# Four graph-attention layers on one core: a small sum moved from GpSimd to ScalarE, a third of one layer's gathers of late rows replaced by matmuls, and a group of transposes moved ahead in TensorE's order

## The chip, the cores and the metric

The kernel runs on one core of a Trainium2 chip. The metric is the device time of one execution in microseconds (us). Engines are named as the profile names them: PE is TensorE (PEld its weight loads), DVE is VectorE, ACT is ScalarE, POOL is GpSimd, and SP is the engine that issues most loads. Times inside an execution are counted from the start of its span.

## The reference, cut to what matters

Four layers follow one another on x, 4096 nodes with 256 features, and on one adjacency matrix (4096 x 4096, some eight neighbours and the node itself in a row). Each layer normalises x, applies max(., 0), and adds an attention result to x:

```python
# layer 0: 8 heads, a curvature term      logits_ij = leaky(e_l[i] + e_r[j]) + gate * curv_bias[i, j]
# layer 1: one head                       e_ij = leaky(a1.h_i + a2.h_j + b)
# layer 2: one head, softmax of e and of -e
attention          =  softmax(where(mask,  e, NEG), axis=1)
negative_attention = -softmax(where(mask, -e, NEG), axis=1)
new_h = concatenate([attention @ inp, negative_attention @ inp], axis=1) @ wtrans
x = x + elu(new_h)
# layer 3: 4 heads, scores h_i . h_j
```

The adjacency matrix is an input, so which rows take part is known only at run time.

## The kernel before, in words

**Lists and gathers.** Layer 0's part of the program reads the whole adjacency matrix (64 MB), packs it to keys and finds, for each tile of 128 nodes, up to 9 chunks of 128 neighbour rows (`EC` = 9). There are 32 tiles. For a tile, every layer fetches the chunks from a table in HBM, one indirect DMA on POOL's queue for each chunk (line 909, `gather`), into a buffer `g` of which there are six (`G`). Chunks 0 to 6 (`EARLY` = 7) reach only table rows below 3584 (`NE`), so they can be fetched as soon as tiles 0 to 27 of the layer before have stored their rows. Chunks 7 and 8 (`LATE` = 8) need the whole table. The node's own row comes as a plain DMA on SP's queue (line 923).

**Expanding instead of gathering.** Chunk 8 holds only rows of the last four tiles (3584 and up). Layers 1 and 3 don't gather it: `keep_late` (line 1676) keeps these 512 rows in SBUF as three bf16 parts, `go_to` (line 1684) has made a 0/1 matrix `to` for each tile, stored in `rows_of` beside the tile's other matrix, and `expanded` (line 1695) multiplies the two in twelve matmuls and copies the result into `g` on ACT. Layer 2 gathers all nine chunks. So there are 32 x (9 + 8 + 9 + 8) = 1088 gathers.

**Layer 0's score.** `before0` (line 1489) spreads a tile's own terms to its edges and writes them to `mine`; its last statement, lines 1503 to 1505, adds `noloop` to the 8 own terms of the node itself, on POOL. `score0` (line 1507) adds `mine` to the gathered terms on DVE (line 1512). `weigh0` (line 1537) weighs the rows on DVE, `attend0` sums them on PE (line 930), `finish0` and `rows1` (line 1563) make the table rows of layer 1.

**Layer 2's steps** are called by `run` (line 1714) in rounds: a pair (lag, step) means that round r runs the step for tile r - lag. In a round PE takes: `attend2` of tile r (28 matmul instructions, line 1921), `turn3` of tile r - 2 (line 865, two transposes), `turn_signed` of tile r - 1 (line 1943, four transposes, copied to `two_t` on ACT, line 1947), `rows3` of r - 2 (line 874) and `through_wt` of r - 1 (line 1956, eight matmuls). `weigh2` makes the weights `sw` on DVE (lines 1777 to 1908); `signed2` takes the reciprocal of attend2's sums (DVE), the factor `scale` (line 1932) and writes `two` on ACT (line 1936). `finish2` ends the tile on DVE, and `rows3` makes layer 3's table rows.

**What sets the order.** PE's order is the order of the program. The other engines' orders are chosen by the scheduler of the framework from a model of costs, so they can change with any edit; each engine then runs its own queue in order. PSUM banks for layer 2's small products (`pt`) number three.

Of the kernel before, what the change touches and what calls it, by code (L numbers as in the profile page):

```python
# [10 lines left out]
BF16 = mybir.dt.bfloat16  # L11
# [3 lines left out]
AF = mybir.ActivationFunctionType  # L15
OP = mybir.AluOpType
# [4 lines left out]
P = 128  # L21
C = 256
KC = C // P
H0, D0, CF = 8, 32, 6
# [673 lines left out]
EC = 9  # L698
HE = 5 * P
SELF = EC  # L700
KX = 8
LATE = EC - 1
EARLY = EC - 2
G = 6
BEHIND = 3
ROW0, ROW1, ROW3 = C + H0 + CF, C + 2, C
# [7 lines left out]
def gnn_lists(  # L714
# [27 lines left out]
    nc = tc.nc  # L742
    N = x_in.shape[0]
    NT = N // P
# [35 lines left out]
    def tile_rows(a, t):  # L780
        return a[t * P : (t + 1) * P, :]
# [24 lines left out]
    LB = (N - NE) // P  # L806

    rows_of = [
        dram.tile([P, 2, (EC + LB) * P], BF16, name=f"rows_of{t}") for t in range(0, NT, 2)
    ]  # L810
# [19 lines left out]
    rows12 = [const.tile([P, 2, ROW1], F32, name=f"row12_{i}") for i in range(2)]  # L830
# [47 lines left out]
    def upper(a):  # L878

        n = len(a.shape)  # L880
        two = a.bitcast(BF16)
        if n == 2:
            return two.rearrange("p (a two) -> p a two", two=2)[:, :, 1]
        return two.rearrange("p s (a two) -> p s a two", two=2)[:, :, :, 1]
# [5 lines left out]
    def fetch(pool, src, shape, name, dtype=F32, bufs=3):  # L890
        a = pool.tile(shape, dtype, name=name, bufs=bufs)
        nc.sync.dma_start(a, src)
        return a
# [13 lines left out]
    def gather(t, g, table, width, chunks):  # L907
        for c in chunks:
            last = nc.gpsimd.indirect_dma_start(  # L909
                out=g[:, c, :width], out_offset=None, in_=table[: NE if c < EARLY else N, :],  # L910
                in_offset=bass.IndirectOffsetOnAxis(ap=nbr[:, t, c : c + 1], axis=0),
            )
        return last
# [7 lines left out]
    def gather_late(t, g, table, width, chunks=range(EARLY, EC)):  # L921
        last = gather(t, g, table, width, chunks)
        nc.sync.dma_start(g[:, SELF, :width], tile_rows(table, t))
        return last
# [25 lines left out]
    def three(a):  # L950

        return a.rearrange("p (b c) k -> p b c k", c=3)


    with tc.tile_pool(name="keep", bufs=1) as keep, tc.tile_pool(
# [9 lines left out]
        g = g_pool.tile([P, EC + 1, ROW0], F32, name="g").rearrange("p c k -> p (c k)")  # L965
# [18 lines left out]
        for e, size in zip(enc, (1.0, 0.5)):  # L984
# [5 lines left out]
                op0=OP.mult, op1=OP.mult,  # L990
# [30 lines left out]
        for i, a_s in enumerate((ar_s, al_s)):  # L1021
            for k in range(KC):
                nc.vector.tensor_scalar(
                    am[:, k, i * H0 + k * nh : i * H0 + (k + 1) * nh], of_head, a_s[:, k : k + 1],
                    None, op0=OP.mult,
# [25 lines left out]
        to = keep.tile([P, 1], F32, name="to")  # L1051
# [7 lines left out]
        noloop = keep.tile([P, NT], F32, name="noloop")  # L1059
        wc_b = keep.tile([EC * CF, EC, H0], F32, name="wc_b")  # L1060
        own0 = keep.tile([P, NT, 3, H0 + CF], F32, name="own0")
# [427 lines left out]
        def before0(t):  # L1489

            ps = ps_b.tile([P, 3, 512], F32, name="pb")
            my = mine0[:, t % MINE, :]
            nc.any.tensor_copy(
                my[:, P:].rearrange("p (i v) -> p i v", i=3), upper(own0[:, t, :, :])
            )
            s_ps, parts = spread(ps, of0[t].pop("st"), my, P + 3 * V0)
            s = of0[t]["s"] = work.tile([P, EC, P], F32, name="s_f", bufs=3)
            nc.scalar.copy(three(s), s_ps)
            mine = of0[t]["mine"] = work.tile([P, EC + 1, V0], F32, name="mine")
            nc.vector.tensor_reduce(  # L1500
                three(mine[:, :EC, :]), parts.rearrange("p b c (i v) -> p b c v i", i=3), AX.X, OP.add
            )
            nc.gpsimd.tensor_scalar(
                mine[:, SELF, :H0], own0[:, t, 0, :H0], noloop[:, t : t + 1], None, op0=OP.add
            )

        def score0(t):
# [89 lines left out]
        for q, n in groups:  # L1597
            for t in range(q, q + n):
                last = at_piece((t // (RG // P) + 1) * per_r - 1) + 7 + 2.5 * (t % (RG // P))
# [5 lines left out]
        first = 17 + NE // P * T_ROWS  # L1605
# [26 lines left out]
    with tc.tile_pool(name="work", bufs=2) as work, tc.tile_pool(name="kept", bufs=1) as kept:  # L1632
# [43 lines left out]
        def keep_late(rows, width):  # L1676

            for b in range(0, LB, 2):
                n = min(LB, b + 2) - b
                row = rows[b // 2 - (LB + 1) // 2][:, 2 - n :, :]  # L1680
                rest = work.tile([P, 2, ROW1], F32, name="rest", bufs=1)[:, :n, :width]
                in_parts([late_rows[:, b : b + n, i, :width] for i in range(3)], row, rest)
# [12 lines left out]
        def expanded(t, of, width, pool, name):  # L1695

            to = of.pop("to")
            ps = bank(pool, name)[:, :width]
            for b in range(LB):
                for i in range(3):  # L1700
                    nc.tensor.matmul(  # L1701
                        ps, lhsT=to[:, b * P : (b + 1) * P], rhs=late_rows[:, b, i, :width],
                        start=(b == 0 and i == 0), stop=(b == LB - 1 and i == 2),
                    )
            nc.scalar.copy(of["g"][:, LATE, :width], ps)
# [5 lines left out]
        def by_slot(a):  # L1711
            return a.rearrange("p (c r) -> p c r", r=P)

        def run(table, width, x_of, steps, first=None, expand=False, rows=True):


            of, late = [{} for _ in range(NT)], {}

            def loads(t):
                two = t // 2 * 2  # L1720
                if t == two:
                    of[t]["ss"] = work.tile([P, 2, EC * P], BF16, name="ss", bufs=3)
                    if not first:
                        nc.sync.dma_start(of[t]["ss"], s_of[t // 2])
                of[t]["pair"] = of[two]["ss"]
                of[t]["s"] = by_slot(of[t]["pair"][:, t - two, :])
                if rows:
                    if t == two:
                        of[t]["sts"] = work.tile([P, 2, (EC + LB) * P], BF16, name="st", bufs=4)
                        if not first:  # L1730
                            nc.sync.dma_start(of[t]["sts"], rows_of[t // 2])
                    both = of[two]["sts"][:, t - two, :]
                    of[t]["st"], of[t]["to"] = both[:, : EC * P], both[:, EC * P :]
                if first:
                    marked(first, t, of[t]["st"])
                    go_to(t, of[t]["to"])
                    if t > two:
                        store(rows_of[t // 2], of[two]["sts"])
                four = t // XT * XT
                if t == four:  # L1740
                    of[t]["xs"] = fetch(work, rows_of_x(x_of, t), [P, XT, C], "x")
                of[t]["x"] = of[four]["xs"][:, t - four, :]
                of[t]["all_x"] = of[four]["xs"]

            def begin(t):
                with ExitStack() as queue:
                    if t - BEHIND in late:
                        queue.enter_context(tc.issue_after(late.pop(t - BEHIND).ins))
                    of[t]["g"] = gather_early(t, table, width, g_pool)

            def begin_late(t):
                last = gather_late(t, of[t]["g"], table, width, range(EARLY, LATE if expand else EC))
                if t < G - BEHIND:
                    late[t] = last

            def late_lag(t):

                return (-1, -2, -2, -3, -3)[t] if t < 5 else 2 - G

            steps = [(-3, loads), (2 - G, begin), (late_lag, begin_late)] + [  # L1760
                (lag, lambda t, f=f: f(t, of[t])) for lag, f in steps
            ]
            rounds = {}
            for lag, f in steps:
                for t in range(NT):
                    rounds.setdefault(t + (lag(t) if callable(lag) else lag), []).append((f, t))
            for r in sorted(rounds):
                for f, t in rounds[r] if r < NT else sorted(rounds[r], key=lambda s: -s[1]):
                    f(t)
# [11 lines left out]
        with tc.tile_pool(name="only1", bufs=2) as only, tc.tile_pool(name="l1_o", bufs=2, space=PSUM) as ps_o, tc.tile_pool(  # L1781
# [7 lines left out]
                    late_no[:, b : b + 1], number, float(NE + b * P), None, op0=OP.add  # L1789
                )  # L1790
            nc.vector.tensor_copy(col_late, nbr[:, :, LATE])
            keep_late([rows12[t // 2 % len(rows12)] for t in range(0, NT, 2)], ROW1)

            def expand1(t, of):
                expanded(t, of, ROW1, ps_e, "pe")
# [46 lines left out]
            def rows2(t, of):  # L1842
# [15 lines left out]
                    (3, give2), (0, weigh1), (2, finish1), (1, attend1), (-1, before1),  # L1858
                    (2, rows2), (-1, expand1),
                ],  # L1860
                first=only, expand=True,
            )

        HP = P // 2
# [13 lines left out]
        with tc.tile_pool(name="only2", bufs=2) as only, tc.tile_pool(name="l2_o", bufs=2, space=PSUM) as ps_o, tc.tile_pool(  # L1878
# [2 lines left out]
            small2 = bank(ps_m, "small2")  # L1881
            all_rows = kept.tile([P, C], F32, name="all_rows")
            nc.vector.memset(all_rows, 0.0)

            def weigh2(t, of):

# [89 lines left out]
            def rows3(t, of):  # L1976
# [19 lines left out]
                for k in range(K3):  # L1996
# [4 lines left out]
            run(  # L2001
                table2, ROW1, xs[1],
                [
                    (0, weigh2), (1, signed2), (2, finish2), (0, attend2), (2, turn3), (1, turn_signed),
                    (2, rows3), (1, through_wt),
                ],
                rows=False,
            )

            ps = bank(ps_t, "pt")[:, :C]  # L2010
# [5 lines left out]
        with tc.tile_pool(name="only3", bufs=2) as only, tc.tile_pool(name="l3_o", bufs=2, space=PSUM) as ps_o, tc.tile_pool(  # L2016
# [69 lines left out]
            def finish3(t, of):  # L2086
# [12 lines left out]
            run(  # L2099
                table3, ROW3, xs[2],  # L2100
                [(0, weigh3), (1, attend3), (-1, before3), (2, finish3), (-1, expand3), (-2, own_parts)],
                expand=True,
            )


# [2 lines left out]
            for i, v in enumerate(inv):  # L2108
# [8 lines left out]
                op0=OP.add, op1=OP.subtract,  # L2117
# [89 lines left out]
```

## Time and profile before

| | |
|---|---|
| median of 3 runs | 1580.23 us (1580.05 to 1581.6) |
| profiled execution: its own time, its span | 1580.64 us, 1578.8 us |
| busy: PE, DVE, ACT, POOL | 1275.2, 1147.6, 686.5, 1076.9 us |
| gathers (line 909): number, busy in all | 1088, 1048.8 us |
| layer 0's gathers: first starts, last ends | 109.43 us, 511.60 us |
| layer 1's gathers | 526.79 us to 852.66 us |
| layer 2's gathers | 852.96 us to 1215.43 us |
| layer 3's gathers | 1217.68 us to 1538.88 us |
| line 1503 (the sum on POOL) | 32 times, median 324 ns |

The profile is one execution. Its groups give, for a line of the kernel, the engine, the tiles written and read, how often it ran, its busy time and the idle time just before it with what ended that. A timeline lists an engine's instructions by time, with the idle time ahead of each in brackets. A table by stretches gives each engine's busy time in a part of the span, with the granted clock of PE. The chain of waits of the page reaches back only to 640 us, so for what lies before that the timelines are read. The first gather of a layer is told from its place in POOL's order (288, 256, 288 and 256 gathers).

### The profile page before, as it was taken

The page shows a single profiled execution, that of the slowest core. Times are in us where ns is not written, and L with a number is a line of the kernel's source. Part 1 is how long each engine was busy: PE and PEld are TensorE (multiplying, and loading weights), DVE is VectorE, ACT ScalarE, POOL GpSimd, SP SyncE. Part 2 cuts the span into 40 slices and gives each one's busy share as a digit, 9 for nine tenths or more (in the row PEclk, how much of TensorE's full clock was granted, in tenths as well). Part 3 has the DMA queues.
Part 4 walks back from the last instruction along what each step waited for, and adds up shares of the span by engine and source line. Part 5 has one row for each costly group of instructions (what it writes and reads, how often), then busy time and mean ns, then how long its engine had stood idle before and what let it go on. Part 6 is the DMA issues. An engine that isn't in the chain of part 4 may idle for free.

```text
span 1578.8 us, 24849 instructions
## 1 busy us (share of the span) xinstructions
PE 1275.2 (81%) x7529; PEld 1026.4 (65%) x7536; DVE 1147.6 (73%) x3171; ACT 686.5 (43%) x1801; POOL 1076.9 (68%) x1179
## 2 busy tenths in 40 slices
PE   5773878877887759867777399989989799999995
PEld 3442656656665648756665378877777588888884
DVE  6666978888885567766665167766666699999995
ACT  4665767787452355544432044443444411111220
POOL 2027767777677477777777777777777777777770
PEclk9965888788898989988888699999999999999998
DMA  8969879998565578877779657766666767777740
GB/s 284 303 232 330 293 262 304 334 329 269 126 156 155 159 230 248 261 225 225 232 221 295 195 163 216 210 201 191 193 207 185 224 207 244 247 252 245 241 123 20
DMA packets 165921, 356.67 MB, mean 226 GB/s; under 512 B 28177, under 2 KB 100241, under 8 KB 165777
## 3 DMA queue, kind: packets, MB, share of 16 engines
q0 software_dynamic: 52224, 145.30, 33.6%
q1 hardware_dynamic: 67970, 143.98, 27.0%
q10 hardware_dynamic: 45582, 65.71, 11.6%
q8 instruction: 62, 1.02, 0.3%
q14 instruction: 83, 0.67, 0.1%
HBM read 291.66 MB, written 63.21 MB: 225 GB/s over the span
## 4 chain that ended last, share of the span: by engine, by line
PE 25%; POOL 11%; DVE 8%; DMA 7%; issue 6%; ACT 2%; DVEq 0%; POOLq 0%; ACTq 0%
POOL g L909 11%; PE o L930 9%; DMA g<-table,nbr 7%; PE o L1921 6%; PE pv L2058 3%; PE pt L1956 3%; DVE g L2076 3%; PE pv L1701 2%; DVE sw L1899 1%; PE pt L874 1%; ACT two_t L1947 0%; DVE prod L1848 0%; PE pt L1943 0%; DVE s L1777 0%; PE pe L1701 0%
## 5 line engine op out<-in xcount | busy, mean ns | idle before, releaser
L909 POOL DMA_INDIRECT g<-table,nbr x1088 | 1048.8, 964 | 374.7 <-issue 300.3
L930 PE MATMUL o<-g,sw 128*128 128x257 f32 (+1 forms) x1216 | 301.0, 405 | 3.0 <-DVE sw L1823 3.0
L930 PEld LDWEIGHTS o<-g,sw 128*128 128x128 f32 x1216 | 243.9, 203 | 43.7 <-DVE sw L1823 3.4
L1921 PE MATMUL o<-g,sw 128*128 128x257 f32 x896 | 204.9, 387 | 25.5 <-issue 25.5
L1921 PEld LDWEIGHTS o<-g,sw 128*128 128x128 f32 x896 | 174.6, 195 | 52.1 <-issue 25.5
L930 PE MATMUL o<-g,s_f 128*128 128x264 f32 x576 | 152.6, 424 | 0.0
L930 PEld LDWEIGHTS o<-g,s_f 128*128 128x128 f32 x576 | 124.7, 216 | 27.3
L1204 ACT ACTIVATE mask<-adj,minus_half 128x1024 bf16<-128x1024 int32 x112 | 125.3, 1144 | 21.0 <-DMA adj<-in_adj_l 9.0
L2067 ACT ACTIVATE pm<-s 128x40 f32<-128x40 f32 x32 | 6.6, 208 | 226.9 <-DVE s L2065 212.5
L2058 PE MATMUL pv<-parts,st 128*128 128x256 bf16 x864 | 101.1, 275 | 1.5 <-DMA parts<-own 1.5
L2062 DVE TENSOR_TENSOR v<-pv,g 128x512 f32<-128x512 f32 (+1 forms) x160 | 90.7, 628 | 4.1 <-PE pv L2058 4.0
L2058 PEld LDWEIGHTS <-st 128*128 128x128 bf16 x864 | 84.9, 98 | 12.7 <-DMA parts<-own 1.9
L2076 DVE SCALAR_TENSOR_TENSOR g<-pm,g 128x2560 f32<-128x2560 f32 x32 | 90.3, 2823 | 2.6 <-ACT g L2072 2.0
L1537 DVE TENSOR_TENSOR g<-g,pt 128x2560 f32<-128x2560 f32 x32 | 90.0, 2813 | 0.4 <-ACT pt L1534 0.3
L1956 PE MATMUL pt<-wt_s,two_t 128*128 128x256 f32 x256 | 69.2, 418 | 20.8 <-ACT two_t L1947 20.5
L898 ACT ACTIVATE off<-place,minus 128x1152 bf16<-128x1152 f16 x64 | 80.0, 1250 | 7.4 <-DVE st L899 5.7
L1701 PEld LDWEIGHTS <-st 128*128 128x128 bf16 x768 | 74.1, 98 | 13.9
L2063 DVE TENSOR_REDUCE s<-v 128x36 f32<-128x2304 f32 x32 | 81.7, 2553 | 1.1
L865 PE MATMUL pt<-ident,r 128*128 128x128 f32 x192 | 43.1, 311 | 47.5 <-DVE r L845 35.8
L874 PE MATMUL pt<-wcat,hT 128*128 128x272 f32 (+1 forms) x256 | 76.0, 423 | 4.6 <-ACT hT L867 4.2
L1956 PEld LDWEIGHTS pt<-wt_s,two_t 128*128 128x128 f32 x256 | 49.9, 202 | 35.5 <-ACT two_t L1947 28.9
L865 PEld LDWEIGHTS pt<-ident,r 128*128 128x128 f32 x192 | 25.8, 157 | 63.4 <-ACT rstd L836 22.5
(360 smaller groups left out, 2259.7 us busy)
## 6 DMA issues: line engine op xcount, KB each, us to landing
adj<-in_adj_l SPq DMA_DIRECT2D x128, 512.0 KB
ss<-s_of SPq DMA_DIRECT2D x32, 576.0 KB
g<-table,nbr POOLq DMA_INDIRECT x1088
rows_of<-st ACTq DMA_DIRECT2D x16, 832.0 KB
st<-rows_of SPq DMA_DIRECT2D x16, 832.0 KB
x<-x SPq DMA_DIRECT2D x24, 512.0 KB
s_of<-ss ACTq DMA_DIRECT2D x16, 576.0 KB
table<-row ACTq DMA_DIRECT2D x32, 258.0 KB
```

The lines of the kernel that those rows point to most:

```text
L874: nc.tensor.matmul(pp, lhsT=hT[:, k, :], rhs=w[:, k, :], start=(k == 0), stop=(k == KC - 1))
L909: last = nc.gpsimd.indirect_dma_start(out=g[:, c, :width], out_offset=None, in_=table[: NE if c < EARLY else N, :], in_offset=bass.Indirec ...
L930: nc.tensor.matmul(o, lhsT=a, rhs=b, start=(i == 0), stop=(i == len(pairs) - 1))
L1204: nc.scalar.activation(m, a, AF.Sign, bias=minus_half, scale=1.0)
L1537: nc.vector.tensor_mul(gh, gh, w[:, :, :, None].to_broadcast([P, K, H0, D0]))
L1701: nc.tensor.matmul(ps, lhsT=to[:, b * P : (b + 1) * P], rhs=late_rows[:, b, i, :width], start=(b == 0 and i == 0), stop=(b == LB - 1 and i ...
L1921: nc.tensor.matmul(o, lhsT=sw[:, h, i].rearrange("p s r -> p (s r)"), rhs=g[:, c, : C + 1], start=(i == 0), stop=(i == HC + 1),)
L1956: nc.tensor.matmul(pp, lhsT=lhs[:, k, :], rhs=wt_s[:, k, :], start=(k == 0), stop=(k == 2 * KC - 1))
L2058: nc.tensor.matmul(pv[:, k, :], lhsT=st[:, (a + k) * P : (a + k + 1) * P], rhs=parts[:, i, :], start=(i == 0), stop=(i == 2),)
L2062: nc.vector.tensor_mul(v[:, a : a + n, :], pv[:, :n, :], g[:, a : a + n, :C])
L2063: nc.vector.tensor_reduce(s[:, :EC, :], heads(v, K3), AX.X, OP.add)
L2076: weighed3[t] = nc.vector.scalar_tensor_tensor(gh, w[:, :, :, None].to_broadcast([P, K, K3, D3]), -math.e, gh, op0=OP.add, op1=OP.mult,)
```

## The change

Three edits.

1. Layer 0's own term is computed by an ACT instruction (Identity with `noloop` as bias) in place of the one on POOL.
2. In layer 2, tiles with t % 3 == 1 (1, 4, ..., 31: eleven tiles) expand chunk 8 on PE and don't gather it. For this `keep_late` runs once more at the start of layer 2, on the last rows of layer 1; `to` is fetched for these tiles by a DMA of 128 x 512 bf16 on SP's queue, in the round three ahead; the twelve matmuls come last in the round two ahead, into a `pt` bank.
3. In layer 2's round `turn_signed` of the tile before stands ahead of `attend2`, and `through_wt` ahead of `rows3`.

```diff
-            nc.gpsimd.tensor_scalar(
-                mine[:, SELF, :H0], own0[:, t, 0, :H0], noloop[:, t : t + 1], None, op0=OP.add
+            nc.scalar.activation(
+                mine[:, SELF, :H0], own0[:, t, 0, :H0], AF.Identity, bias=noloop[:, t : t + 1],
+                scale=1.0,
             )
...
             def begin_late(t):
-                last = gather_late(t, of[t]["g"], table, width, range(EARLY, LATE if expand else EC))
+                last = gather_late(t, of[t]["g"], table, width, range(EARLY, LATE if expand(t) else EC))
...
-            keep_late([rows12[t // 2 % len(rows12)] for t in range(0, NT, 2)], ROW1)
+            last12 = [rows12[t // 2 % len(rows12)] for t in range(0, NT, 2)]
+            keep_late(last12, ROW1)
...
             nc.vector.memset(all_rows, 0.0)
+            keep_late(last12, ROW1)
+
+            def by_tensor(t):
+                return t % 3 == 1
+
+            def fetch_to(t, of):
+                if by_tensor(t):
+                    of["to"] = fetch(
+                        only, rows_of[t // 2][:, t % 2, EC * P :], [P, LB * P], "to", BF16, bufs=3
+                    )
+
+            def expand2(t, of):
+                if by_tensor(t):
+                    expanded(t, of, ROW1, ps_t, "pt")
...
-                    (0, weigh2), (1, signed2), (2, finish2), (0, attend2), (2, turn3), (1, turn_signed),
-                    (2, rows3), (1, through_wt),
+                    (0, weigh2), (1, signed2), (2, finish2), (1, turn_signed), (0, attend2), (2, turn3),
+                    (1, through_wt), (2, rows3), (-2, expand2), (-3, fetch_to),
                 ],
-                rows=False,
+                rows=False, expand=by_tensor,
```

In layers 1 and 3 `expand` becomes a function that is always true, which changes nothing there.

More of the change, by code (lines that the diff above doesn't have):

```diff
@@ L1712, in by_slot, with run @@
             return a.rearrange("p (c r) -> p c r", r=P)
-        def run(table, width, x_of, steps, first=None, expand=False, rows=True):
+        def run(table, width, x_of, steps, first=None, expand=lambda t: False, rows=True):
             of, late = [{} for _ in range(NT)], {}
@@ L1860, in gnn_lists @@
                 ],
-                first=only, expand=True,
+                first=only, expand=lambda t: True,
             )
@@ L2101, in gnn_lists @@
                 [(0, weigh3), (1, attend3), (-1, before3), (2, finish3), (-1, expand3), (-2, own_parts)],
-                expand=True,
+                expand=lambda t: True,
             )
```

## The prediction

> **What bounds the kernel now.** By the table of stretches PE looks like layer 2's bound (90 to 97% busy from 893 to 1200 us, POOL 76%). POOL's timeline, read next, says otherwise. Here layer 2's last gathers meet layer 3's first:
>
> ```profile
> 1213.23 0.95 POOL L909 DMA_INDIRECT g<-table,nbr  x1 [0.30 <-issue]
> 1214.48 0.95 POOL L909 DMA_INDIRECT g<-table,nbr  x1 [0.30 <-issue]
> 1217.68 0.94 POOL L909 DMA_INDIRECT g<-table,nbr  x1 [2.25 <-DVE r L845]
> ```
>
> A gather takes 0.95 us and the next follows 0.30 us later, whose releaser is "issue": nothing the profile shows is waited for. So 0.30 us belongs to a gather's price, 1.25 us, and POOL is full at "76%". Layer 2's 288 gathers run from 852.96 to 1215.43 without one longer gap: 362.5 us, 1.259 each. Layer 1's 256 (325.9 us) and layer 3's (321.2 us) run on in the same way. From 526.8 us to 1538.9 us POOL waits only about 2 us, above, for layer 2's tile 27 to store its rows. From about tile 13 on, attend2 starts follow POOL: from 1021.95 (tile 13) to 1224.11 (tile 31) one each 11.23 us, where nine gathers cost 11.3.
>
> Layer 0 is different. POOL ends there at 511.60 and layer 1's first gather starts at 526.79: it waits for tile 27's table rows, whose `rows1` ends at 523.01 (line 1563) and whose store is issued at 523.04. So compute sets that layer's end. DVE's and PE's timelines tell what it waited for:
>
> ```profile
> 491.72 0.22 DVE L1510 TENSOR_TENSOR d<-g,mine 128x54 f32<-128x54 f32 x1 [0.17 <-DVE e L1532]
> 499.95 0.24 DVE L1512 TENSOR_TENSOR e<-g,mine 128x80 f32<-128x80 f32 x1 [8.01 <-POOL mine L1503]
> 500.23 0.24 DVE L1513 SCALAR_TENSOR_TENSOR e<-e 128x80 f32<-128x80 f32 x1
> 500.38 2.81 DVE L1537 TENSOR_TENSOR g<-g,pt 128x2560 f32<-128x2560 f32 x1
> ```
>
> ```profile
> 505.45 0.66 PE L865 MATMUL pt<-ident,r 128*128 128x128 f32 x2 [7.88 <-DVE r L845]
> 506.04 0.70 PE L1524 MATMUL pt<-wc_b,d_t 54*128 54x72 f32 x2
> 506.67 1.25 PE L930 MATMUL o<-g,ident 128*128 128x264 f32 x2
> 507.71 6.06 PE L930 MATMUL o<-g,s_f 128*128 128x264 f32 x18
> ...
> 517.40 4.17 PE L930 MATMUL o<-g,s_f 128*128 128x264 f32 x18
> ```
>
> The sum on POOL takes 0.32 us, but it stands behind gathers in POOL's queue. DVE waits 8.01 us for it, everything behind it on DVE waits too, and PE stands 7.88 us; the 18 matmuls after that take 6.06 us instead of 4.17.
>
> **Part 1, the self term.** In all DVE waits for line 1503 five times:
>
> ```profile
> L1503 POOL TENSOR_SCALAR mine<-own,noloop x32: 297/324/876, 21.0 to 511.9; 128x8 f32<-128x8 f32 x32
> ...
> who waited for it (us, times):
>   DVE e L1512: 25.3, 5
> ```
>
> Two of the five (11.4 us, after 430 us) lie in the tail that ends layer 0, three (13.9 us) earlier. *Tail*: without the 8.01 us, e ends at 492.2, the weighing (2.81) at 495.2; attend of tile 26 ends at 495.93, finish0 takes 2.2 us of DVE after it, so PE's transposes start at 498.1 and the next attend, 1.22 us after them, at 499.3 instead of 506.67: 7.4 us. The attend is then as short as the others: 4.7 instead of 7.1 us, 2.4 more. Of the second stall (3.38 us at 476.75) PE shows waits of 1.44 and 0.96; I take half, 1.2. Tail: 11.0 us, between 0 and 13.8. The granted clock was 0.76 in the 10 us with PE's wait, 0.65 in the 8 us after it and 1.00 in the 16 us after those. The Trainium skill's page "TensorE: Matmul & The Clock Gate" (Part 1) says that an idle window of about 3.4 us halves the clock until some 3.4 us of work have passed; by its rule alone the slow matmuls would cost 1.7 us and not the measured 2.4, and the sum would be 0.7 smaller.
>
> *Earlier*, ACT, DVE and PE wait for one another around the adjacency pieces. The groups of four tiles end their ranking (line 1252) 54.5 and 53.0 us apart where stalls of 6.1 and 5.3 us lie, and 45.9 to 49.2 (mean 47.3) in the later four. That speaks for up to 13; against it, the DMA engines are 86 to 88% busy. A stall removed from one engine of a convoy is mostly found again at the next, so I take 3.5, a quarter; the ends are 13.9 and, for the 24 or so added ACT instructions of 0.26 us (the row of line 1283, same shape) all exposed, a loss of 6. POOL itself gains 0.23 us for each sum taken out between gathers, which the wait at 511.6 hides. Part 1: **14.5 us**. Everything after it starts that much earlier, since layer 1's gathers start with tile 27's store; their other condition, tile 31's rows before the 29th gather, has 8 us to spare.
>
> **Part 2, the expansion.** Eleven gathers leave POOL: 11 x 1.259 = 13.8 us. What it adds:
>
> ```profile
> L1701 PE MATMUL pe<-late_rows,st x384: 270/274/423, 563.9 to 849.7; 128*128 128x258 bf16 x192
> ...
> L1705 ACT COPY g<-pe x32: 353/374/382, 567.3 to 855.7; 128x258 f32<-128x258 f32 x32
> ```
>
> Twelve such matmuls stand in the chain of waits as 1.34 us: 11 x 1.34 = 14.7 us of PE, 0.46 a tile. ACT's eleven copies of 0.37 us and SP's eleven loads of 128 KB are hidden: ACT is 44% busy there, and SP runs over two rounds (20 us) ahead. Uncovered, the copies cost 4.1 us, the loads up to 2.8 each (the longer landings of gathers in the chain). `keep_late` is two times (ACT 0.61, DVE 0.69, ACT 0.62, DVE 0.69), 5.2 us; DVE idles 23.49 us until layer 2's first gathers land (892.31), and that hides it. The first attend (894.07) follows 30 gathers that stay.
>
> Does PE now set the pace? A round of layer 2, in the chain's order, is attend 6.07, turn3 0.22, turn_signed 0.44, rows3 1.13, through_wt 1.73: 9.59 us. With 0.46 it is 10.05, against POOL's 362.5 less 13.8 over 32, 10.90. PE begins late, since it fills while POOL is already 40 us in. From attend of tile 2 at about 912.8 (below), 29 rounds give tile 31 at 1204. By the gathers its score, now at 1218.67, comes at 1204.9 and the attend some 4.5 us later, 1209.4. So gathers still decide, by 5 us, and the whole 13.8 us arrive. It may not exceed this, since POOL then runs on into layer 3.
>
> **Part 3, the order.** Now, when a gather is late, `two` of the tile before waits on DVE behind the late tile's weights, `two_t` waits behind `two` in ACT's queue, and PE waits for it before it can start the late attend:
>
> ```profile
> PE o L1921 <- issue: 25.5, 1, 25.5
> PE pt L1956 <- ACT two_t L1947: 19.1, 11, 2.3
> ```
>
> The 25.5 us are the layer's start, before the first attend. In the new order the 19 us go. What is late next is `two` itself, ahead of turn_signed: it ends 2.1 us after an attend where gathers are early (939.75 to 941.84), and turn3, through_wt and rows3 (3.08 us) cover it; 4 to 4.5 us where they are late, when PE waits for the gather anyway. At the layer's start nothing covers it: tile 1's attend starts 2 us later and tile 2's at 912.8, not 914.06. Since POOL sets the pace, I count part 3 as nothing for the end (between a loss of 2 and a gain of 1). It keeps PE from becoming the bound. `rows3` of tile 27, which layer 3's first gather awaits, moves behind through_wt, 1.3 us later in its round; attend being up to 14.7 us earlier, the gather is still 13.8 earlier.
>
> **Sum.** 1580.64 (the profiled execution; its span 1578.8 and 1.8 around it) - 14.5 - 13.8 = 1552.3; that execution is 0.4 above the median of the runs, so I say **1552**. Layer 3 keeps its length: PE and DVE are 98% busy there from 1350 to 1450, and it moves as one piece.
>
> **Rivals.**
> *A, the self term waits on ACT instead.* ACT runs its queue in order, and in 100 to 430 us it stood 43.4 us (15 times, at most 6.5) for PE ahead of line 1563. If the new instruction sits behind such a wait, DVE's 25.3 us come back. For: ACT waited some 98 us there in all. Against: the copy `s_f` just before it in the program is seldom late (2.3 us of DVE waits). Time: 1580.6 - 13.8 = 1567. The Trainium skill's page "TensorE: Matmul & The Clock Gate" (its note on engine queue depths) calls ACT's queue strictly first-in, first-out; by that rule this rival is possible at any wait of ACT, and the trace agrees (`two_t` behind `two`).
> *B, PE becomes layer 2's bound.* If PSUM's three banks or ACT's queue add 0.6 us to a round, 31 rounds of 10.65 are just today's 330 us from attend 0 to attend 31: part 2 brings nothing. For: PE has 8% to spare. Time: 1580.6 - 14.5 = 1566.
> *C, slower: turn_signed stalls PE in each round.* The place is `two` ahead of attend. If ACT takes the expansion's copy and rows3's work ahead of `two`, it ends 4.5 us after attend, as now in late rounds, and exceeds the cover of 3.08 by 1.4. Then 31 x (10.05 + 1.4) = 355, 25 more than 330; less 14.5 it is 1591. It decides from 1.06 us a round. Against it: only a third of the rounds have such a copy.
> *D, more:* all of the early 13.9 us arrive too: 1542.
>
> **Chances.** Forecast 0.55, A 0.13, B 0.12, D 0.09, C 0.11 (with lesser losses of new queue orders). The unknown costs make the forecast's own range 1544 to 1562; with A, B and D's upper part it is **1541 to 1571**, about 8 in 10. A run tells 0.2% (3 us) from no change: faster 0.87, same 0.03, slower 0.10.
>
> **What would show it.** Right: no DVE wait for line 1503's result; layer 1's first gather near 512; layer 2's gathers 277 in about 349 us without gaps; PE's waits for `two_t` gone; layer 3's first gather near 1189. Wrong: DVE waiting for ACT at line 1512 (A); gaps among layer 2's gathers, which then wait for buffers (B); PE waiting for `two` ahead of line 1943 in most rounds (C).

## The result, and the profile after

The kernel after takes **1542.76 us** (median of five runs, 1541.17 to 1545.98); the kernel before, 1580.23 (five runs, 1579.99 to 1582.56). The ratio is 0.9765, interval 0.9749 to 0.9781: 37.5 us less, where 28 were forecast and where rival D stood (1542). The profiled execution took 1542.87, its span 1541.2. The granted clock is 0.903 (before 0.894).

| us | before | after | moved |
|---|---|---|---|
| layer 0's gathers end | 511.60 | 498.72 | -12.9 |
| layer 1's first gather | 526.79 | 504.04 | **-22.8** |
| layer 2's first gather | 852.96 | 829.89 | -23.1 |
| layer 2's gathers end | 1215.43 | 1179.98 | -35.5 |
| layer 3's first gather | 1217.68 | 1181.17 | **-36.5** |
| layer 3's gathers end | 1538.88 | 1502.89 | -36.0 |
| span ends | 1578.8 | 1541.2 | -37.6 |

So layer 0 gave 22.8 us (14.5 forecast), layers 1 and 2 together 13.75 between the two bold rows (13.8 forecast), the rest about 1. These are figures of one execution of each kernel; four more executions of the same layer 0 are set beside them below.

POOL's timeline after, where layer 1 and layer 3 begin (start, length, what ran, idle time ahead and its releaser):

```profile
497.77 0.95 POOL L909 DMA_INDIRECT g<-table,nbr  x1 [0.30 <-issue]
504.04 0.94 POOL L909 DMA_INDIRECT g<-table,nbr  x1 [5.32 <-PE o L930]
...
1179.04 0.95 POOL L909 DMA_INDIRECT g<-table,nbr  x1 [0.30 <-issue]
1181.17 0.94 POOL L909 DMA_INDIRECT g<-table,nbr  x1 [1.19 <-PE o L1937]
```

The wait ahead of layer 1 was 15.2 us and is 5.3; the one ahead of layer 3 was 2.25 and is 1.19. Layer 2's 277 gathers take 350.1 us, 1.264 each, with no longer gap.

DVE's timeline after, tile 26, the one that waited 8.01 us before:

```profile
478.76 0.22 DVE L1511 TENSOR_TENSOR d<-g,mine 128x54 f32<-128x54 f32 x1 [0.17 <-DVE e L1533]
478.89 0.23 DVE L1513 TENSOR_TENSOR e<-g,mine 128x80 f32<-128x80 f32 x1
```

The second row has no bracket: nothing is waited for. And PE's timeline around the same attend of tile 26 and the next:

```profile
478.80 4.17 PE L930 MATMUL o<-g,s_f 128*128 128x264 f32 x18
...
485.35 0.41 PE L865 MATMUL pt<-ident,r 128*128 128x128 f32 x2 [0.74 <-ACT rstd L836]
485.69 0.44 PE L1525 MATMUL pt<-wc_b,d_t 54*128 54x72 f32 x2
486.05 0.71 PE L930 MATMUL o<-g,ident 128*128 128x264 f32 x2
486.61 4.17 PE L930 MATMUL o<-g,s_f 128*128 128x264 f32 x18
...
919.38 6.23 PE L1937 MATMUL o<-g,sw 128*128 128x257 f32 x28
925.46 0.38 PE L865 MATMUL pt<-ident,r 128*128 128x128 f32 x2
925.67 1.89 PE L1972 MATMUL pt<-wt_s,two_t 128*128 128x256 f32 x8
927.40 1.03 PE L874 MATMUL pt<-w_s,hT 128*128 128x256 f32 x4
928.27 1.50 PE L1702 MATMUL pt<-late_rows,to 128*128 128x258 bf16 x12
929.61 0.60 PE L1959 MATMUL pt<-ident,two 128*128 128x128 f32 x4
930.04 6.23 PE L1937 MATMUL o<-g,sw 128*128 128x257 f32 x28
```

Ahead of the next attend PE waits 0.74 us instead of 7.88, and the attend takes 4.17 us like its neighbours instead of 6.06. The lower half is one round of layer 2 in the new order, with an expansion (the 1.50 us row): from attend to attend 10.66 us; without one it is 9.32.

PE's waits in layer 2 (870 to 1195 us: who waited, for whom, us in all, times, longest):

```profile
PE o L1937 <- issue: 17.8, 1, 17.8
PE pt L1959 <- ACT two L1952: 8.8, 8, 1.7
PE pt L874 <- ACT hT L867: 1.3, 2, 0.9
PE pt L1972 <- ACT two_t L1963: 0.8, 2, 0.6
```

The 19.1 us for `two_t` are 0.8 now, and `two` is late next, eight times, as forecast. Rounds run at PE's own 9.32 and 10.66 us until about tile 18, where PE catches up with POOL; after that the gathers set the pace.

### The profile page after: what moved, and what is told of

Read it like the earlier page. It is cut to its first block, busy times and chain, and to the rows that moved or that the text cites. A ratio compares the mean times of both kernels' runs of the same rounds, so it can differ in the third digit from the quotient of the medians.

```text
span 1541.2 us, 25111 instructions
## 1 busy us (share of the span) xinstructions
PE 1277.0 (83%) x7668; PEld 1032.4 (67%) x7668; DVE 1136.6 (74%) x3177; ACT 691.1 (45%) x1846; POOL 1050.8 (68%) x1136
## 4 chain that ended last, share of the span: by engine, by line
PE 45%; DMA 13%; DVE 13%; POOL 12%; issue 8%; ACT 4%; ACTq 0%; DVEq 0%; POOLq 0%; SPq 0%
PE o L930 20%; POOL g L909 12%; DMA g<-table,nbr 9%; PE o L1937 9%; PE pv L2074 3%; PE pt L874 2%; DVE g L2092 2%; PE pt L1972 2%; PE pv L1702 2%; DMA table<-row 1%; PE pt L865 1%; PE pt L1702 1%; PE pt L1959 1%; PE pt L1525 1%; DVE g L1538 1%
## 5 line engine op out<-in xcount | busy, mean ns | idle before, releaser
L909 POOL DMA_INDIRECT g<-table,nbr x1077 | 1035.0, 961 | 365.5 <-issue 302.0
L930 PE MATMUL o<-g,sw 128*128 128x257 f32 (+1 forms) x1216 | 304.5, 408 | 2.7 <-DVE sw L1825 2.7
L930 PE MATMUL o<-g,s_f 128*128 128x264 f32 x576 | 156.0, 431 | 0.0
L1702 PEld LDWEIGHTS <-st 128*128 128x128 bf16 x768 | 74.2, 98 | 13.8
L874 PE MATMUL pt<-wcat,hT 128*128 128x272 f32 (+1 forms) x256 | 72.6, 407 | 4.3 <-ACT hT L867 4.0
L867 ACT COPY hT<-pt 128x256 f32<-128x256 f32 x96 | 35.4, 369 | 65.2 <-PE pt L865 62.3
L930 PE MATMUL o<-g,ident 128*128 128x264 f32 (+1 forms) x128 | 52.5, 498 | 13.9 <-DVE g L2092 12.5
```

Of the source, the lines that this page charges most:

```text
L874: nc.tensor.matmul(pp, lhsT=hT[:, k, :], rhs=w[:, k, :], start=(k == 0), stop=(k == KC - 1))
L909: last = nc.gpsimd.indirect_dma_start(out=g[:, c, :width], out_offset=None, in_=table[: NE if c < EARLY else N, :], in_offset=bass.Indirec ...
L930: nc.tensor.matmul(o, lhsT=a, rhs=b, start=(i == 0), stop=(i == len(pairs) - 1))
L1702: nc.tensor.matmul(ps, lhsT=to[:, b * P : (b + 1) * P], rhs=late_rows[:, b, i, :width], start=(b == 0 and i == 0), stop=(b == LB - 1 and i ...
```

## Where layer 0's 22.8 us come from

Ranking ends for a group of four tiles with line 1254 on DVE. The time from one group's end to the next:

| group | before | stall in it (wait for line 1503) | after |
|---|---|---|---|
| 2 | 51.8 | | 50.5 |
| 3 | 54.9 | 6.14 us at 143.89 | 49.1 |
| 4 | 52.7 | 5.32 us at 205.74 | 45.7 |
| 5 | 49.1 | 2.45 us at 246.66 | 48.7 |
| 6 | 46.6 | | 46.1 |
| 7 | 48.7 | | 49.8 |
| 8 | 45.5 | | 46.5 |

The gain is 5.8 and 7.0 us in just the two groups with the long stalls. Up to the end of group 4 DVE runs the same instructions in the same order in both traces (its order first differs at 231.97 us before, 217.09 after), so no new order of the scheduler stands behind these two gains. For what follows DVE's and ACT's orders differ too, and no run separates what that gave.

The last group ends 13.6 us earlier. Of these, 2.1 us were there when group 2 ended (123.30 to 121.24), ahead of the first stall; groups 3 to 5 add 13.2, for stalls of 13.9; groups 6 to 8 give 1.6 back.

The tail is counted by the first row of an attend. Tile 24's, before and then after:

```profile
472.65 0.71 PE L930 MATMUL o<-g,ident 128*128 128x264 f32 x2
```

```profile
461.71 0.71 PE L930 MATMUL o<-g,ident 128*128 128x264 f32 x2
```

Tile 24 is 10.9 us earlier (another 2.7 given back), tile 26 13.0 (491.21 to 478.25), tile 27 20.6 (506.67 to 486.05) and tile 28 22.9 (516.85 to 493.94). So the tail adds 2.0 for the stall of 3.38 us, 7.7 for that of 8.01, and 2.3 for the matmuls that no longer run slowly after the pause.

Runs e9 to e12 below hold the same layer 0, with the same order on every engine, and ran on another chip on which the kernel before takes about as long as here. Their layer 1 begins at 506.41, 505.77, 509.59 and 508.29 us. Against the one trace of the kernel before, the five executions thus give 17.2 to 22.8 us, and the one shown is the one with the most. The tail is alike in all five: from tile 24's attend to tile 28's there are 31.9 to 32.2 us, where before had 44.2. What differs lies ahead of it. Tile 24 is 5.4 to 10.9 us earlier; counted from the end of group 2, ahead of the first stall, 6.4 to 8.9. So of the early 13.9 us about a half to two thirds reach the tail.

## The experiments

The first eight runs fell on two chips where the kernel before itself takes 2070 us (e1 to e4) and 2064 us (e5 to e8), so each is compared only with the kernel before on its own chip, and no absolute time of their expectations can be met. Runs e9 to e12 are from a chip where the kernel before takes 1578.64 (eleven runs, 1573.59 to 1584.87). The ratios come with the runs and aren't the quotients of the medians shown.

**e1, the first edit alone; e2, the other two alone; e3, first and second; e4, first and third.** All as changes to the kernel after:

```diff
 e1: both edits below of e3 and e4
 e2:
-            nc.scalar.activation(mine[:, SELF, :H0], ..., AF.Identity, bias=noloop[:, t : t + 1], scale=1.0)
+            nc.gpsimd.tensor_scalar(mine[:, SELF, :H0], ..., noloop[:, t : t + 1], None, op0=OP.add)
 e3:
-  (1, turn_signed), (0, attend2), (2, turn3), (1, through_wt), (2, rows3), (-2, expand2), (-3, fetch_to),
+  (0, attend2), (2, turn3), (1, turn_signed), (2, rows3), (1, through_wt), (-2, expand2), (-3, fetch_to),
 e4:
-            keep_late(last12, ROW1)
-  (1, through_wt), (2, rows3), (-2, expand2), (-3, fetch_to),
+  (1, through_wt), (2, rows3),
-  rows=False, expand=by_tensor,
+  rows=False,
```

> The first edit alone: the self term on ScalarE, layer 2 as before. Theory (every stall of DVE behind the sum on POOL's queue arrives in full at layer 0's end): layer 1's first gather at 504 instead of 526.8, time 1557.5 us. Rival 1 (only the stalls of layer 0's tail count, as forecast, and the rest of the gain came with layer 2's edits): 1566 to 1569 us.

> The second and third edit with the self term left on POOL. Theory (POOL's eleven gathers of 1.26 us are the gain, and it adds to the first edit's): 1565.5 us, layer 2's gathers 277 in 350 us. Rival 1 (the edits help one another): 1558 to 1562 us, since the first edit alone would then bring less.

> The changed kernel with PE's old order in layer 2's rounds: first and second edit. Theory (POOL sets the pace, PE has room in either order): within 2.5 us of the changed kernel, 1543 to 1545.5 us, and PE's waits for two_t are back (some 10 to 20 us). Rival 2 (the new order is what makes room on PE for the expansion; with the old one a round is near 10.9 us): 1550 us or more, and gaps among layer 2's gathers.

> The changed kernel without the expansion: first and third edit, all nine chunks gathered in layer 2. Theory: the 13.8 us of POOL come back, 1556.5 us, PE's rounds 9.3 us while it isn't waiting for gathers. Rival 2 (the order brings a good part of the gain): 1547 to 1551 us.

| | median us | ratio to before | interval | layer 2's gathers take |
|---|---|---|---|---|
| e1: edit 1 | 2063.94 | 0.9979 | 0.9946 to 1.0012 | 443.0 us |
| e2: edits 2, 3 | 2048.03 | 0.9885 | 0.9851 to 0.9918 | 421.8 us |
| e3: edits 1, 2 | 2046.56 | 0.9889 | 0.9831 to 0.9947 | 432.9 us |
| e4: edits 1, 3 | 2049.06 | 0.9922 | 0.9892 to 0.9952 | 435.2 us |

None of the four tells what an edit gives on a chip like the first. Edit 1 alone gives nothing clear of noise here (between 11 us less and 2.5 more). The trace of e2, which has the sum on POOL as the kernel before has, shows why:

```profile
L1503 POOL TENSOR_SCALAR mine<-own,noloop x32: 303/325/762, 21.4 to 686.2; 128x8 f32<-128x8 f32 x32
its engine sat idle before it (us, times) until:
  DVE e L1512: 16.7, 2
...
who waited for it (us, times):
busy tenths in 40 slices 0000000000000000000000000000000000000000
```

Under "who waited for it" nobody is listed: POOL waits here for DVE, and DVE never for this sum. Each tile's sum ends at least 5.6 us before DVE's line 1512, which reads it, starts. So on this chip there was no stall for edit 1 to take away, and e1 speaks neither for nor against its theory on a chip like the first.

PE's waits over the whole span, in e3 (old order) and then in e4 (new order):

```profile
PE pt L1972 <- ACT two_t L1963: 42.1, 19, 14.1
```

```profile
PE pt L1971 <- ACT two_t L1962: 1.5, 1, 1.5
```

The new order, and not the expansion, takes away the wait for `two_t`; e2, with the new order, has 3.3 us of it, e1, with the old, 46.8. In its place PE waits for `two`, 32.0 us in e2 and 8.8 in e4. On this chip POOL pauses about 2 us in nearly every round (13.3 us long in e1), so it isn't the bound there. Against e1, layer 2's gathers take 7.8 us less with the order and 10.1 with the expansion, one execution each; layer 1, with the same program in all four, takes between 388.4 and 400.5, so neither is shown. Both edits together are clearer: 418.3 to 421.8 us in e2, e7 and e8, 438.7 to 443.0 without them in e1, e5 and e6.

**e5 and e6, the first edit for half of the tiles** (layer 2 as before):

```diff
+            if t < NT // 2:      # e5; e6: t >= NT // 2
                 nc.scalar.activation(mine[:, SELF, :H0], ...)
+            else:
+                nc.gpsimd.tensor_scalar(mine[:, SELF, :H0], ...)
```

> The first edit for tiles 0 to 15 alone, layer 2 as before: ScalarE adds the self term there, POOL for tiles 16 to 31. Theory (early stalls, 13.9 us at tiles 1, 5 and 8, arrive in full): 1566 to 1567 us, if the scheduler leaves the stalls of tiles 26 and 28 as they were. Rival 1 (the convoy of the adjacency phase swallows three quarters of them): 1576 to 1577 us.

> The first edit for tiles 16 to 31 alone, layer 2 as before. Theory (the tail's two stalls cost 8 to 11 us): 1569 to 1572 us. Rival 1 (the tail carries nearly all of the 22.8 us): 1558 to 1562 us.

Measured: e5 2051.81, 0.9962 (0.9923 to 1.0001); e6 2063.18, 0.9996 (0.9965 to 1.0028). Neither differs clearly from the kernel before, and the split of layer 0's gain into early and tail isn't settled by them: in both traces, too, DVE never waits for the sum, wherever it is computed. It is POOL that waits once for DVE, 6.5 us in e5 and 9.6 in e6.

**e7 and e8, the kernel after with some 14 us of extra work in tiles 0 to 15 of layer 0**, on DVE and on ACT, its result unused:

```diff
+            if t < NT // 2:
+                for i in range(2):
+                    junk = work.tile([P, C], F32, name="junk", bufs=1)
+                    nc.vector.tensor_mul(junk, g[:, i, :C], g[:, i + 1, :C])                  # e7
+                    nc.scalar.activation(junk, g[:, i, :C], AF.Copy, scale=1.0)               # e8
```

> The changed kernel with two more multiplications of 128x256 (0.42 us each, result unused) on DVE for tiles 0 to 15 of layer 0: 13.6 us of DVE. Theory (in the adjacency phase a microsecond of DVE is a microsecond of the kernel): 1553 to 1556 us. Rival 1 (DMA or ScalarE sets the pace there, DVE's time is mostly slack): 1543 to 1547 us.

> The changed kernel with two more copies of 128x256 (about 0.47 us each, result unused) on ScalarE for tiles 0 to 15 of layer 0: about 15 us of ACT. Theory (DVE is the pace-maker, ACT at 70 to 76% has room): 1543 to 1548 us. Rival 3 (ACT, which converts the adjacency pieces, paces this phase as much): 1554 us or more.

Measured: e7 2040.67, 0.9899 (0.9834 to 0.9963); e8 2044.68, 0.9906 (0.9875 to 0.9938). The kernel after didn't run on that chip, so what the load costs there is unknown. Inconclusive.

**e9, e10, e11: half, two thirds and all of layer 2's tiles expanded.**

```diff
-                return t % 3 == 1
+                return t % 2 == 1      # e9: 16 tiles; e10: t % 3 != 0, 21 tiles; e11: True, 32 tiles
```

> The changed kernel with every second tile of layer 2 expanded (16 instead of 11). Theory: POOL sheds five more gathers, 6.3 us, and PE's mean round becomes 9.32 + 0.67 = 9.99 us, so that tile 31's attend would be at 1180 by PE and 1183.5 by the gathers: 1536 to 1538 us. Rival B (PE is already the bound): 1543 us or more.

> Tiles with t % 3 != 0 expanded (21). Theory: POOL sheds ten more gathers than the changed kernel (12.6 us), but PE's mean round is 9.32 + 0.88 = 10.20 us, tile 31's attend at 1186 by PE: PE decides, 1538 to 1541 us. Rival (POOL alone decides at every share): 1530 us.

> All 32 tiles of layer 2 expanded. Theory: PE's round is 10.66 us, from 890 for tile 2 to 1199 for tile 31, 9 us after the changed kernel's 1189.8: 1550 to 1553 us, though POOL sheds 21 gathers more. Rival (POOL alone decides): 1516 us.

**e12, the kernel after without the expansion's matmuls**:

```diff
-                    expanded(t, of, ROW1, ps_t, "pt")
+                    of.pop("to")
+                    nc.scalar.copy(of["g"][:, LATE, :ROW1], late_rows[:, 0, 0, :ROW1])
```

> The changed kernel with the eleven expansions' 132 matmuls left out (ACT copies rows of a kept part in their place, so chunk 8 of these tiles is not the neighbours' rows). Theory (the matmuls are hidden, since gathers decide layer 2's end): 1541 to 1543 us. Rival B (PE's 14.7 us are paid): 1530 to 1535 us.

| | after | e9 | e10 | e11 | e12 |
|---|---|---|---|---|---|
| tiles expanded | 11 | 16 | 21 | 32 | 11, no matmuls |
| median, us | 1542.76 | 1537.97 | 1548.36 | 1561.46 | 1542.53 |
| ratio to before | 0.9765 | 0.9742 | 0.9818 | 0.9892 | 0.9769 |
| interval | 0.9749 to 0.9781 | 0.9718 to 0.9766 | 0.9793 to 0.9843 | 0.9865 to 0.9918 | 0.9743 to 0.9796 |
| POOL ends layer 2 | 1179.98 | 1178.50 | 1168.9 | 1158.1 | 1185.8 |
| layer 3's first gather | 1181.17 | 1180.90 | 1180.36 | 1196.87 | 1189.10 |
| last attend of layer 2 | 1189.78 | 1187.55 | 1187.49 | 1204.35 | 1194.66 |
| layer 2's first gather to layer 3's | 351.3 | 346.7 | 348.4 | 360.3 | 353.6 |
| kernel's last row (SP's store) | 1532.55 | 1531.52 | 1530.52 | 1548.47 | 1537.02 |
| span ends | 1541.2 | 1539.5 | 1546.4 | 1563.5 | 1545.2 |

The rows below the interval are of one profiled execution each, in e9, e11 and e12 the slowest of its runs; layer 0 alone ends up to 5.6 us apart in them, so layer 2 is best compared by its own row.

e12 agrees with the expectation: without 132 matmuls, 14.7 us of PE, the ratio to before is the same (the kernel after ran on another chip). Layer 2's gathers take 350.4 us there and 350.1 after. The matmuls are hidden in the kernel after. e9 agrees too, and is the fastest of all, though its ratio's interval overlaps that of the kernel after; five gathers fewer make layer 2 4.6 us shorter. e10 and e11 show the other bound. POOL's timeline at the start of layer 3, first e10, then e11:

```profile
1180.36 0.94 POOL L909 DMA_INDIRECT g<-table,nbr  x1 [11.48 <-PE o L1937]
```

```profile
1196.87 0.94 POOL L909 DMA_INDIRECT g<-table,nbr  x1 [38.73 <-DVE parts L1675]
```

POOL is done 11 and 39 us early and waits for rows that PE's rounds make: tile 27's store is issued at 1177.11 and 1193.97, some 3 us before these gathers. In e11 every round is 10.66 us from tile 2 on, without a wait; the last, with nothing left to expand, is 9.32. In e10, too, all rounds from tile 3 on have PE's own length, and in e9 all but one, of 12.72 us ahead of tile 30. So the two engines are about level at 16 expanded tiles, and at 21 PE is layer 2's bound. That doesn't yet make 21 worse than 11: layer 2 takes 348.4 us there, against 351.3 after.

Both also took 7 us and more longer than expected, and most of that isn't in layer 2. In e10 the last row of the kernel comes 2 us earlier than after and the span ends 5 us later (table).

What follows that row is in the trace's records of the sequencers, which the views leave out: POOL closes with an instruction named DRAIN, 1.47 us after, 9.31 in e10, 8.41 in e11. From the last row to the end of the span is 8.6, 15.9 and 15.0 us. Without the difference (7.3 and 6.4 us) e10 would be, as an estimate, at 1541.1 and e11 at 1555.1, against 1538 to 1541 and 1550 to 1553 expected.

## Why the prediction was right, and where it was too small

The kernel got faster by the two mechanisms forecast, and by more. The time lies 1.2 us below the forecast's own range (1544 to 1562); only the wider one, drawn for rival D, holds it. No run on a chip like the first has one edit alone, so what follows is read from the traces.

- **The early stalls: the term that was too small.** "A stall removed from one engine of a convoy is mostly found again at the next, so I take 3.5, a quarter." In five executions the tail's first attends come 5.4 to 10.9 us earlier, 6.4 to 8.9 counted from the end of group 2. From the end of group 2 to the end of group 5 11.5 to 13.2 of the 13.9 arrive; then part of that is indeed lost again, but what is missing at the tail is a third to a half of the 13.9 and not three quarters. The forecast had the evidence: the two groups with the long stalls were 54.9 and 52.7 us long (it read 54.5 and 53.0), against a mean of 47.5 in the later four, "up to 13". The counter-argument, DMA engines 86 to 88% busy, was a share of busy time and named no wait that would end last in the stall's place.
- **The tail** was forecast at 11.0 and is 12.0 (2.0 + 7.7 + 2.3), up to 12.3 in the later runs. The stall of 8.01 us gave 7.7, for 7.4; the one of 3.38 gave 2.0, for 1.2. The slow matmuls gave 2.3, as the forecast's own reading had it (2.4), and not the 1.7 that it worked out from the Trainium skill's page "TensorE: Matmul & The Clock Gate" (Part 1), with 3.4 us of work at half the clock. The trace before shows a granted clock of 0.50 from 502 to 511 us and through 505.5 to 511.5, when PE was busy again without a break: 6 us of work ran at half the clock. In the kernel after the granted clock is 1.00 from 450 to 505 us.
- **The expansion** was forecast at 13.8. Layer 2's gathers are 12.4 us shorter (362.5 to 350.1: eleven fewer, each a little longer apart), the wait ahead of layer 3 is 1.1 shorter, and between layers 1 and 2 there are 0.3. That PE's extra matmuls cost nothing is shown by e12, and that PE soon would be the bound by e10. A round is 9.32 or 10.66 us, not 9.59 and 10.93.
- **The order** counted as nothing for the end. That it removes the wait for `two_t` is shown by e3 and e4. Whether the kernel after would lose time with the old order on a chip like the first wasn't tried.
- **The end**, not in the sum: from the last gather to the end of the span there are 1.7 us less. Up to the kernel's last row it is 0.9 more (28.8 to 29.7), behind it 2.6 less (11.2 to 8.6), where POOL's DRAIN shrank from 2.36 to 1.47 us.
- **The rivals.** A fell: no wait of DVE for line 1503, whose 32 runs on ACT take 0.29 us each. B fell for eleven tiles and holds for 21. C fell: `two` is waited for eight times, 8.8 us in all, once at the layer's start and otherwise from 1057 us on, where the gathers set the pace. D, given 0.09, has the right time (1542) for partly the wrong reason: not all of the early 13.9 us arrived, and a larger tail, a shorter end and 2.1 us from ahead of the first stall made up for it.

## What to carry to other kernels

Where the groups of a loop are longer exactly where a stall lies, and by its length, give that difference weight: here 11.5 to 13.2 of 13.9 us had come back by the end of the third such group, and 6.4 to 8.9 were left some 200 us later. Keep small work that another engine waits for out of a queue of long transfers: a sum of 0.32 us on POOL cost this kernel 17 to 23 us by the traces. Look first whether anyone waits, though: on the slower chip of e2, whose DVE never waited for that sum, moving it gave nothing measurable. When work is moved from a full engine to a second one, work out at how many pieces the second is full; here the two are about level at 16 of 32, which also had the lowest time.

## What the runs showed of the hardware that was not expected

- **The end of the program goes with the number of indirect DMAs, with a step.** POOL's closing DRAIN took 2.36 us with 1088 gathers, 1.47 with 1077, 1.06 with 1072, then 9.31 with 1067 and 8.41 with 1056: about 0.082 us for each gather, and a step of 8.7 us between 1072 and 1067. The chip and the other edits don't matter: every run with 1088 gathers had 2.36, every one with 1077 had 1.47, on whichever chip. The two counts behind the step were run in one kernel each. Why there is a step stays open.
- **Two chips ran this program 30% slower.** In e1 and e4 a gather took the same 0.95 us, and 1.25 from start to start inside a round, but engines stood where no releaser is shown. PE's waits in layer 1 (700 to 1000 us) in e4, of a stream of matmuls that has no such wait in the kernel after:

```profile
PE pe L1702 <- issue: 25.2, 39, 1.9
```

  Thirty-nine waits of up to 1.9 us between consecutive matmuls. Over the whole of e4 the mean granted clock was 0.81 and the DMA moved 174 GB/s, against 0.90 and 230 in the kernel after. Why, stays open.
